# A graph network in four layers: layer 3's source factors by a way through DRAM instead of by two wide products per chunk

## The chip, the cores and the metric

The kernel runs on one core of a Trainium2 chip. The metric is the device time of one execution in microseconds (us); less is better. A core has five engines with their own instruction queues: TensorE (PE, the matrix products; PEld is its weight load), VectorE (DVE), ScalarE (ACT), GpSimd (POOL) and SyncE (SP), which here only issues transfers. An engine works off its own queue in order and waits for the others through semaphores.

## The reference

2708 nodes have 128 features each, and a sparse weighted adjacency of 2708 x 2708 in float32 with a full diagonal. Four layers each normalise the rows, cut them at 0, and add the layer's result to x. Layers 2 and 3 are those that matter:

```python
# layer 2
h = jnp.maximum(_layernorm(x), 0.0)
agg = adj @ h
msg = relu(agg @ W_msg.T + b_msg)
x = x + gru_cell(msg, h, W_ih, W_hh, b_ih, b_hh)
# layer 3
h = jnp.maximum(_layernorm(x), 0.0)
x_norm = _ln(h, g1, b1)
mask = (adj > 0) | eye
for i in range(2):
    hh = x_norm @ ff0_w[i].T
    s_src = hh @ attn_w[i, :c]
    s_dst = hh @ attn_w[i, c:]
    e = leaky_relu(s_src[:, None] + s_dst[None, :])
    e = where(mask, e, NEG)
    att = softmax(e, axis=1) @ hh + h
    att = _ln(att, g2, b2)
    h_next = h_next + elu(att @ ff1_w[i].T) / 2
x = x + h_next
```

With slope 0.01 the leaky ReLU is a maximum of two lines, so the exponential of a score splits into factors of source and destination. For source i and destination j the weight, up to a factor of i alone that the softmax takes out again, is mask x max(exp(-0.99 s_src[i]), exp(0.99 s_dst[j])) x exp(0.01 s_dst[j]). The kernel needs exp(-0.99 s_src[i]) along the free axis, the same on all 128 partitions, because there j lies on the partitions and i along the free axis. This is the tile `row`, the subject of the change.

## The kernel before

The 2708 nodes are 22 tiles of 128 (the last has 20). Layers 0 and 1 come first; layer 0 also writes the transposed adjacency to DRAM (`adjT`), and layer 1 works on lists of each node's neighbours. The changed part begins with layer 2.

Layer 2 goes over chunks of four tiles of destination nodes (`GROUPS`, six chunks, five of 512 columns and one of 148). `aggregate` (L941 to L963) takes a chunk's adjacency in five pieces of up to five row tiles, loads each with `nc.sync.dma_start` (L947, L949) into one of three buffers `a2`, makes from it the byte mask that layer 3 will use (L951 on VectorE, L954 on GpSimd), and adds its products up in PSUM (L959). So 22 products per chunk, five for each piece of 1.28 MB but two for the last. A buffer is free for the piece three later when its products and both masks have read it.

What else has to be done for a chunk is `finish_chunk` (L965 to L1060), a Python generator: the recurrent cell (L979 to L1009), its transposed result p_y (L1015), two normalisations (`moments`, `factors`, `scale_rows`), the transposed rows zT (L1034), then the source rows, then for each tile one product p_hv with `w_x` (L1050), which gives both heads' features and the four attention scores, with the exponentials of the destination scores (`hv`, `lift`), a copy of all four scores (`score`, used to flag sizes too large) and the scaled features (L1056).

The order of all instructions is written out by hand (`manual_schedule`). A software clock, `spend`, counts TensorE work, one unit for a product of 512 columns; `follow` enrols a generator, and `advance` resumes each at the point that its last `yield n` asked for, n units later. So the parts of chunk g's `finish_chunk` come to lie between the adjacency products of chunk g+1 and partly g+2, and each engine receives its instructions in the order in which Python emits them. This holds for SyncE too: a transfer stands in its queue where it was emitted, between the loads of pieces. The banks that `bank` hands out (p_h, p_z, p_m, p_row, p_hv, p_y) are two in turn.

The source rows before: `src_w` (L284) holds the source weights of a head copied along 128 columns, so that one product with zT gives the same source scores on all 128 partitions, and ScalarE writes their exponential to `row` (L1040 to L1045).

Layer 3's main part is `products` (L812): for each run of output tiles (`RUNS`: 3, 8, 8 and 3 tiles), each of the 22 source row tiles j and each head, `weigh` has VectorE make the weights from `row`, `lift` and `mask` (L806), and TensorE multiplies them (L838). The first run is interleaved with the last parts of `finish_chunk` for chunks 4 and 5; the part between the last adjacency product and the end of those chunks is called the seam below.

Layer 1 already uses a store followed by a read to all partitions: `pass_on` writes `passed` to DRAM (L443) and reads it back with `partition_broadcast` (L445).

Of the kernel before, what the change touches and what calls it, by code (L numbers as in the profile page):

```python
# [20 lines left out]
F32 = mybir.dt.float32  # L21
BF16 = mybir.dt.bfloat16
AF = mybir.ActivationFunctionType
# [7 lines left out]
P = 128  # L31
N = 2708
D = 128
# [18 lines left out]
def size(t):  # L52
    return min(P, N - t * P)
# [7 lines left out]
def listed_layers(ctx: ExitStack, tc: tile.TileContext, x, adj, w, out, flag):  # L61
    nc = tc.nc
# [4 lines left out]
    wdram = ctx.enter_context(tc.tile_pool(name="wdram", bufs=2, space=bass.MemoryType.DRAM))  # L67
    ps = ctx.enter_context(tc.tile_pool(name="ps", bufs=2, space=PSUM))

    def bank(name):  # L70
        return ps.tile([P, CH], F32, tag="ps", name=name)
# [12 lines left out]
    ident = const.tile([P, P], F32, name="ident")  # L84
# [60 lines left out]
    def span(t, k):  # L145

        return t * P, min(k * P, N - t * P)
# [12 lines left out]
    late = ctx.enter_context(tc.tile_pool(name="late", bufs=1))  # L160
# [36 lines left out]
    with tc.tile_pool(name="l0c", bufs=1) as fix:  # L197
# [4 lines left out]
        with (  # L202
# [6 lines left out]
            for gi, (g0, gk) in enumerate(GROUPS):  # L209
# [4 lines left out]
                for q in range(gk):  # L214
                    n = g0 + q
# [28 lines left out]
                for j in range(NT):  # L244
                    k = size(j)
                    p = bank("p_T")
# [34 lines left out]

    NX = 2 * D + 4
    w_x = late.tile([P, NX], F32, name="w_x")
    src_w = late.tile([P, 2, P], F32, name="src_w")  # L284

    def layer3_weights():
        nc.vector.tensor_copy(w_x[:, 0 : 2 * D], ff0T)
        for k in range(2):
            p = bank("p_w")[:, 0:2]
            nc.tensor.matmul(p, ff0[:, k, :], attn[:, 2 * k : 2 * k + 2], start=True, stop=True)  # L290
            nc.vector.tensor_copy(w_x[:, 2 * D + k : 2 * D + k + 1], p[:, 1:2])
            nc.vector.tensor_copy(w_x[:, 2 * D + 2 + k : 2 * D + 3 + k], p[:, 0:1])
        for k in range(2):
            nc.vector.tensor_copy(src_w[:, k, :], w_x[:, 2 * D + 2 + k : 2 * D + 3 + k].to_broadcast([P, P]))

# [470 lines left out]
    row = l3.tile([P, 2, N], F32, name="row")  # L768
    score = l3.tile([P, NT, 4], F32, name="score")
# [15 lines left out]
    def spend(units):  # L785
        clock[0] += units
# [147 lines left out]
    with (  # L934
# [30 lines left out]
        def finish_chunk(t0, k0, pa):  # L965

            c, n = span(t0, k0)
            u = n / CH
# [10 lines left out]
            p = bank("p_m")  # L979
# [31 lines left out]
            p = bank("p_y")  # L1011
# [21 lines left out]
            zT = zpool.tile([D, CH], F32, name="z3T")  # L1033
# [3 lines left out]
            )  # L1037
            spend(u)
            yield 2
            for k in range(2):  # L1040
                p = bank("p_row")
                nc.tensor.matmul(p[:, 0:n], src_w[:, k, :], zT[:, 0:n], start=True, stop=True)
                nc.scalar.activation(row[:, k, c : c + n], p[:, 0:n], AF.Exp, scale=-0.99)
                spend(u)
            yield 1  # L1045
            for q in range(k0):
                t = t0 + q
                m = size(t)
                p = bank("p_hv")
                nc.tensor.matmul(p[0:m, 0:NX], zT[:, q * P : q * P + m], w_x, start=True, stop=True)  # L1050
                spend(0.6)
                nc.scalar.activation(hv[0:m, t, :, D], p[0:m, 2 * D : 2 * D + 2], AF.Exp, scale=0.01)
                nc.scalar.activation(lift[0:m, t, :], p[0:m, 2 * D : 2 * D + 2], AF.Exp, scale=0.99)
                nc.scalar.copy(score[0:m, t, :], p[0:m, 2 * D : NX])
                for k in range(2):
                    nc.vector.tensor_scalar(  # L1056
                        hv[0:m, t, k, 0:D], p[0:m, k * D : (k + 1) * D], hv[0:m, t, k, D : D + 1], None, ALU.mult
                    )
                ready.add(t)
                yield 1  # L1060

        for g, (t0, k0) in enumerate(GROUPS):
            pa = accs.tile([P, CH], F32, tag=f"acc{g % 2}", name="p_agg")
            for j0 in range(0, NT, PIECE):
                aggregate(t0, k0, pa, j0)
            if t0 == 0:
                layer3_weights()
            follow(finish_chunk(t0, k0, pa))
            advance()
# [487 lines left out]
```

## Time and profile before

| | |
|---|---|
| time, median of 3 executions | 1110.71 us (1109.0 to 1111.08) |
| profiled execution, span | 1108.1 us |
| TensorE busy | 963.6 us (87%) |
| VectorE, ScalarE, GpSimd busy | 839.4, 504.2, 394.1 us |
| TensorE clock granted, mean | 0.933 |
| layer 2 with the source rows | about 646 to 811 us |
| seam | about 811 to 863 us |
| rest of layer 3 | about 863 to 1100 us |

The profile is that of one execution. "Busy" is the time in which an engine had an instruction at work; a product of float32 leaves two records. A wait is named by the instruction that ended it: "PE att L838 <- DVE wt L806" means that TensorE stood before the products of line 838 until VectorE's line 806 was done. PEclk is the granted share of TensorE's clock: at 0.50 each product takes twice as long. In a timeline each line has a start, a length, engine, line, operation, output and inputs, and in brackets the idle time ahead with what ended it. Since engines overlap, only the time before the engine that sets the pace counts.

### The profile page before, as it was taken

What the parts mean: (1) busy time and instruction counts of PE and PEld (TensorE: products, weight loads), DVE (VectorE), ACT (ScalarE), POOL (GpSimd) and SP (SyncE); (2) the same over time, 40 slices, a digit from 0 to 9 for tenths busy, and PEclk for the clock granted to TensorE, in tenths of its full rate; (3) what the DMA queues carried; (4) which work ended last, traced back from release to release, by engine and by line L of the source; (5) the groups of instructions that cost most, each with busy time, mean ns of one, the idle gap of its engine ahead of it and who ended that gap; (6) DMA issues with size and microseconds to landing.
All of it is one profiled execution on the core that took longest, in us unless ns stands there. A gap on an engine that the chain in (4) does not pass through costs nothing. (4 is left out here: it accounts for less than half of the span.)

```text
span 1108.1 us, 21904 instructions
## 1 busy us (share of the span) xinstructions
PE 963.6 (87%) x7968; PEld 760.1 (69%) x7968; DVE 839.4 (76%) x2948; ACT 504.2 (46%) x1319; POOL 394.1 (36%) x466
## 2 busy tenths in 40 slices
PE   3998887944389999999999979999979999999993
PEld 1455444523389999999898934444468899999772
DVE  5999999997766668676887255655578977997673
ACT  3857556623476666656676521433322200230142
POOL 4111111103385655776566253344310200340132
PEclk9999889755699999999999989999989999999996
DMA  9488978522133222322222056545300000000000
GB/s 361 164 299 281 324 259 288 178 64 68 46 106 102 96 86 90 106 86 101 83 103 80 28 193 209 190 157 198 100 18 1 1 9 1 1 20 1 2 15 14
DMA packets 55298, 125.39 MB, mean 113 GB/s; under 512 B 7414, under 2 KB 19782, under 8 KB 52472
## 3 DMA queue, kind: packets, MB, share of 16 engines
q1 hardware_dynamic: 48590, 121.12, 31.6%
q10 hardware_dynamic: 6590, 2.77, 1.0%
q8 instruction: 64, 1.05, 0.4%
q14 instruction: 54, 0.44, 0.1%
HBM read 77.30 MB, written 30.84 MB: 98 GB/s over the span
## 5 line engine op out<-in xcount | busy, mean ns | idle before, releaser
L838 PE MATMUL att<-hv,wt 128*128 128x129 f32 (+2 forms) x1936 | 240.7, 281 | 9.2 <-DVE wt L806 9.2
L838 PEld LDWEIGHTS att<-hv,wt 128*128 128x128 f32 (+2 forms) x1936 | 221.8, 190 | 26.2 <-DVE wt L806 9.1
L806 DVE SCALAR_TENSOR_TENSOR wt<-row,lift,mask 128x1024 f32<-128x1024 f32 (+5 forms) x176 | 160.0, 939 | 34.2 <-PE att L838 34.2
L423 POOL TENSOR_SCALAR put<-mine,value 128x128 f32<-128x128 bf16 x176 | 147.7, 855 | 72.4 <-DVE mine L339 70.0
L499 PE MATMUL p_m<-s,sel 128*128 128x128 bf16 x1452 | 160.8, 219 | 5.4 <-ACT g L511 5.4
L119 POOL TENSOR_TENSOR n_r<-n_r,minus_half 128x4 f32<-128x4 f32 (+1 forms) x36 | 51.3, 1425 | 316.1 <-DVE n_r L118 305.2
L503 PE MATMUL p_m<-d,cols 124*128 124x128 bf16 (+1 forms) x1452 | 161.0, 219 | 1.4 <-DVE cols L453 1.3
L220 PE MATMUL acc<-a,hs 128*128 128x512 f32 (+2 forms) x264 | 122.3, 599 | 27.6 <-DMA a<-in_adj 18.9
L524 PE MATMUL agg<-put,g 128*128 128x128 f32 (+1 forms) x968 | 135.8, 281 | 0.0
L241 DVE FIND_INDEX8 col<-val,a 128x8 uint16<-128x124 f32 (+1 forms) x441 | 118.6, 280 | 0.0
L959 PE MATMUL p_agg<-a,hs 128*128 128x512 f32 (+2 forms) x264 | 111.5, 564 | 7.7 <-DVE u L572 4.8
L524 PEld LDWEIGHTS agg<-put,g 128*128 128x128 f32 x968 | 118.1, 192 | 0.0
L499 PEld LDWEIGHTS <-sel 128*128 128x128 bf16 x1452 | 103.7, 97 | 10.8 <-issue 7.1
L503 PEld LDWEIGHTS <-cols 124*128 124x128 bf16 (+1 forms) x1452 | 101.8, 97 | 1.9 <-DVE cols L453 1.9
L240 DVE MAX8 val<-a 128x8 f32<-128x124 f32 (+1 forms) x441 | 102.6, 272 | 0.0
L511 ACT ACTIVATE g<-p_m 128x512 f32<-128x512 f32 x132 | 73.0, 553 | 63.6 <-PE p_m L503 63.6
L431 ACT ACTIVATE put<-mine,value 128x128 f32<-128x128 bf16 x308 | 100.5, 390 | 0.0
L220 PEld LDWEIGHTS acc<-a,hs 128*128 128x128 f32 (+1 forms) x264 | 49.7, 209 | 72.2 <-issue 43.4
L249 PEld LDWEIGHTS p_T<-ident,a 128*128 128x128 f32 x484 | 59.0, 146 | 52.8 <-ACT aT L253 25.4
L249 PE MATMUL p_T<-ident,a 128*128 128x128 f32 x484 | 77.7, 293 | 18.3 <-DMA a<-in_adj 10.0
L253 ACT ACTIVATE aT<-p_T 128x512 f32<-128x512 f32 (+2 forms) x132 | 70.9, 541 | 40.0 <-issue 16.3
L959 PEld LDWEIGHTS p_agg<-a,hs 128*128 128x128 f32 (+1 forms) x264 | 48.6, 196 | 56.6 <-issue 55.1
(228 smaller groups left out, 1396.6 us busy)
## 6 DMA issues: line engine op xcount, KB each, us to landing
a<-in_adj SPq DMA_DIRECT2D x21, 1354.0 KB
adjT<-aT SPq DMA_DIRECT2D x105, 256.0 KB
a<-adjT SPq DMA_DIRECT2D x20, 1280.0 KB
spread<-passed SPq DMA_DIRECT2D x22, 704.0 KB
later<-sel SPq DMA_DIRECT2D x22, 616.0 KB
later<-sel SPq DMA_DIRECT2D x22, 82.5 KB
adjT<-aT SPq DMA_DIRECT2D x21, 74.0 KB
a<-adjT SPq DMA_DIRECT2D x4, 370.0 KB
```

The costliest lines, as they stand in the source:

```text
L220: nc.tensor.matmul(accs[ci][:, 0:cw], h[0:m, n, :], a[0:m, c : c + cw], start=(n == 0), stop=(n == NT - 1))
L240: nc.vector.max(val[:, n, b, :], ab)
L241: nc.vector.max_index(col[:, n, b, :], val[:, n, b, :], ab)
L249: nc.tensor.transpose(p[0:k, q * P : q * P + m], a4[0:m, q, j * P : j * P + k], ident[0:m, 0:m])
L423: nc.gpsimd.tensor_scalar(st["put", 0][:, b, :], st["mine"][:, b, :], st["value"][:, b : b + 1], None, ALU.mult)
L431: nc.scalar.activation(st["put", 1][:, b - HP, :], st["mine"][:, b, :], AF.Identity, scale=st["value"][:, b : b + 1])
L499: nc.tensor.matmul(p[:, b - b0, :], st["sel"][:, b, :], s3[:, q, t % 2, :], start=(q == 0), stop=False)
L503: nc.tensor.matmul(p[:, b - b0, :], st["cols"][0:kb, b, :], d3[0:kb, b, q, :], start=False, stop=(q == 2))
L524: nc.tensor.matmul(agg, g[:, b - 4 * k, :], put, start=(b == 0), stop=False)
L806: nc.vector.scalar_tensor_tensor(wt[0:kj, :], row[0:kj, k, c : c + n], lift[0:kj, j, k : k + 1], mask[0:kj, j, c : c + n], op0=ALU.max, op ...
L838: nc.tensor.matmul(banks[s // 3][0:m, s % 3, :], wt[0:kj, q * P : q * P + m], hv[0:kj, j, k, :], start=(v < 2 and s // 3 not in touched), ...
L959: nc.tensor.matmul(pa[:, 0:n], h[0:k, j, :], a[0:k, j - j0, 0:n], start=(j == 0), stop=(j == NT - 1))
```

## The change

It no longer makes the source rows by products. `p_hv` gives the source scores of each node already, one node per partition, in `score`. The changed kernel takes their exponential for a whole chunk in one small operation (128 x 8), turns it by one transpose, copies it from PSUM, stores the 8 x 128 values to DRAM, and reads them back twice, once per head, to all 128 partitions. The `yield` lines set how far the steps lie apart on the software clock; the transfers go through SyncE's queue. The purpose is to take work off TensorE within layer 2. `src_w` and its copies are no longer needed.

```diff
@@ layer3_weights @@
-    src_w = late.tile([P, 2, P], F32, name="src_w")
...
-        for k in range(2):
-            nc.vector.tensor_copy(src_w[:, k, :], w_x[:, 2 * D + 2 + k : 2 * D + 3 + k].to_broadcast([P, P]))
@@ finish_chunk @@
             spend(u)
             yield 2
-            for k in range(2):
-                p = bank("p_row")
-                nc.tensor.matmul(p[:, 0:n], src_w[:, k, :], zT[:, 0:n], start=True, stop=True)
-                nc.scalar.activation(row[:, k, c : c + n], p[:, 0:n], AF.Exp, scale=-0.99)
-                spend(u)
-            yield 1
             for q in range(k0):
...
                 ready.add(t)
                 yield 1
+
+            own_e = zpool.tile([P, 8], F32, name="own_e")
+            nc.scalar.activation(
+                own_e[:, 0 : 2 * k0].rearrange("p (k t) -> p k t", k=2),
+                score[:, t0 : t0 + k0, 2:4].rearrange("p t k -> p k t"), AF.Exp, scale=-0.99,
+            )
+            yield 2
+            p = bank("p_row")
+            nc.tensor.transpose(p[0 : 2 * k0, 0:P], own_e[:, 0 : 2 * k0], ident)
+            turned = zpool.tile([8, P], F32, name="own_T")
+            nc.scalar.copy(turned[0 : 2 * k0, :], p[0 : 2 * k0, 0:P])
+            yield 2
+            passed = wdram.tile([8, P], F32, name="own_d")
+            nc.sync.dma_start(passed[0 : 2 * k0, :], turned[0 : 2 * k0, :])
+            yield 6
+            for k in range(2):
+                nc.sync.dma_start(
+                    row[:, k, c : c + n],
+                    passed[k * k0 : (k + 1) * k0, :].rearrange("t i -> (t i)")[0:n].partition_broadcast(P),
+                )
```

## The prediction

> **What bounds the kernel now.** I read the page's slices first, then busy time by stage, then TensorE's and SyncE's instructions in the stage the change touches, then who waits for whom. By stage (the window 646 to 811 us is layer 2 with the source rows; columns: length, then busy PE, PEld, DVE, ACT, POOL, granted clock, DMA share, GB/s):
>
> ```profile
> 646.00:811.00 165.00, 159.66 (x442) 76.27 (x442) 97.30 (x269) 54.14 (x140) 68.62 (x45) 0.97 0.51 170
> ```
>
> TensorE works 159.66 of 165 us, nothing else is over 60%, and DMA is half idle. The order of TensorE's work inside that stage (start, length, line, instruction, records; each f32 product leaves two records):
>
> ```profile
> 708.49 1.02 PE L959 MATMUL p_agg<-a,hs 128*128 128x512 f32 x2
> 709.35 1.88 PE L1042 MATMUL p_row<-z3T,src_w 128*128 128x512 f32 x4
> 711.07 1.02 PE L959 MATMUL p_agg<-a,hs 128*128 128x512 f32 x2
> ...
> 715.30 0.61 PE L1015 MATMUL p_y<-ident,y 128*128 128x128 f32 x4
> 715.74 1.02 PE L959 MATMUL p_agg<-a,hs 128*128 128x512 f32 x2
> 716.68 0.68 PE L1050 MATMUL p_hv<-w_x,z3T 128*128 128x260 f32 x2
> 717.19 13.04 PE L959 MATMUL p_agg<-a,hs 128*128 128x512 f32 x30
> ```
>
> From start to start a pair p_row (L1042) takes 1.72 us, one adjacency product (L959) 0.86 (15 from 717.19 to 730.07), one transpose 0.11 (four p_y in 0.44). So TensorE bounds this stage as long as the pieces of adjacency (1.28 MB, five products each) arrive in time. They all come through SyncE's queue, in order. Its waits (line, released by: total us, times, longest):
>
> ```profile
> SPq L947 <- PE p_agg L959: 92.6, 23, 13.5
> SPq L947 <- DVE mask L951: 48.0, 18, 17.1
> ...
> SPq L445 <- DMA passed<-where_T: 25.2, 22, 2.7
> ```
>
> The reader is to see that a load waits for a free buffer, in SyncE, and not for DMA: with three buffers it goes out two pieces ahead. The third line is a store read back through DRAM in layer 1, the pattern that the change adds: the read waits 25.2/22 = 1.1 us for the store.
>
> What a late piece costs is to be seen once, at the start of layer 2, where one load went out only when its buffer came free:
>
> ```profile
> 659.72 3.48 SPq L947 DMA_DIRECT2D a<-adjT  x2
> ...
> 665.70 8.13 PE L959 MATMUL p_agg<-a,hs 128*128 128x512 f32 x14 [2.85 <-DMA a<-adjT]
> 673.77 0.61 PE L290 MATMUL p_w<-attn,ff 128*128 128x2 f32 x4
> ...
> 667.00:670.00 3.00, 3.00 (x4) 1.10 (x4) 1.75 (x3) 0.18 (x1) 2.48 (x2) 0.51 0.86 330
> ```
>
> Issue at 659.72, first product at 665.70: 6.0 us. And the seven products after the 2.85 us gap took 8.07 us to the next start, not 7 x 0.86 = 6.02: 2.05 us more, with the clock at 0.51.
>
> **What the Trainium skill says.** DMA: Bandwidth & Descriptors, section Anatomy of one DMA: "any semaphore wait happens on the issuing sequencer before dispatch". It stands there for GpSimd's path; the waits of SyncE above show the same. TensorE: Matmul & The Clock Gate, section What's actually happening: after an idle window of some 3.4 us the clock is halved, and as long a busy window restores it. The trace agrees: 0.51 after a gap of 2.85 us, 0.50 for 816 to 820 us after one of 4.07 us. No price of the skill is used below, since the trace has each.
>
> **The change part by part.**
> *Removed products.* Two wide products per chunk, six chunks: 1.72 us each for chunks 0 to 4, 0.50 for the narrow chunk 5 (850.64 to 851.14). Chunks 0 to 3 lie in the TensorE-bound stage: 6.9 us. Chunks 4 and 5 lie in the seam after it: 2.2. The exponentials over 128x512 (0.60 us, ScalarE) and two copies (0.22, VectorE) fall away beside other work.
> *Added transposes.* Six of 0.11 us: 0.45 in layer 2, 0.2 in the seam. The two tiny ScalarE operations (0.17 and 0.25, by the rows of score and where_T) are hidden by adjacency products.
> *What the removal does not bring.* The head projections p_hv move up, but they share two banks, and p_y waits for the bank of the third. In the built program VectorE does hv of tiles 1 and 2, y three times (0.69 each), hv of 3 and 4, then p_y is possible. In chunk 0 a table load (1.28 us at 710.2) moves in front of the first hv as well. Step by step I get p_y at 716.2 and the next product's end at 717.5, against 718.05: 0.55 us gained, not 1.6. For the other three 1.45 to 1.8. So layer 2 gains 5.3 us, not 6.4.
> *Seam.* In the built order GpSimd does the last 20-row mask ahead of a power. Before, the first weights waited 1.48 us for that mask (814.92), and TensorE 4.07. I take 1.0 for this and 1.5 for the removed products, where VectorE is nearly as full as TensorE; together 2.5, bounds 0 and 4.
> *The added wait.* This decides. The order of SyncE's queue in the built program, for chunks 0, 1 and 2 alike: load of piece 1, store own_d, load of piece 2, both rows, load of piece 3. The store waits for ScalarE's own_T, that for the transpose, and the transpose stands on TensorE behind the second of piece 1's five products. So load 2, which now goes out two pieces ahead (at 701.4 for use at 720.65), is held until TensorE has done two fifths of piece 1. From the transpose's start T: 0.3 to ScalarE (its usual lag behind p_hv is 0.31), 0.25 its copy (where_T), then the store's issue 0.35: load 2 goes out at T+0.9, and its products can begin at T+6.9. TensorE has left 0.11 + 3 x 0.86 = 2.7 us in chunks 0 and 2, and 3.1 in chunk 1, where p_y comes after the transpose. It idles 4.2, 3.8 and 4.2: 12.2 us. Chunk 3's store comes after the last load, those of 4 and 5 in the seam, and nothing that is urgent stands behind them.
> *Clock.* Each gap is longer than the 2.85 us that halved the clock. Lost: 1.7 (3.4 us at half) to 2.2 (after the gap of 4.07, from 815.76 to 820.1); I take 2.0, three times 6.0.
> *The rows' own transfers.* 0.52 MB at the 390 to 417 GB/s that such a read has in layer 1: 1.3 us. With load 3 behind it, piece 3 is there at T+11.6 (6.9 + 1.3 + 1.28 MB in 3.4), and piece 2 is done at T+11.2 with a full clock, later with half: 0 to 0.4 us each, taken as 0. Chunk 0's rows are first read at 815 us, the others' behind 860: no reader waits.
> *Sum.* -5.3 - 2.5 + 12.2 + 6.0 = +10.4; 1110.7 + 10.4 = 1121.
>
> **Rivals.**
> *Stalls, but a full clock.* If the gaps fall so that no window is idle enough, 6.0 falls away: 1115. For it: a gap of 2.1 us at 308 left the clock alone. Against it: these are twice as long.
> *Deeper stalls.* Piece 3 comes late too, and VectorE, whose mask of piece 2 now stands ahead of the normalisation's factors, delays p_z: some 2 us per chunk more, 1127. For it: the factors do follow that mask in VectorE's order. Against it: I count p_z's input ready at T+17.3, while TensorE gets there at T+17.4 or later.
> *Faster: the wait is hidden.* If load 2 is not held, or lands before its use, only the gains stay: 6.4 + 2.0 + 1.5 for the mask = 9.9, 1101. For it: TensorE is the bound and DMA half idle, and load 2, out at 701.4, is due 13 us before its use. Against it: that slack is from issuing two pieces ahead, which the queue's order takes away, and one load needs 6.0 us where 2.7 remain.
>
> **How the numbers follow.** Forecast with half clock 0.60, full clock 0.20, deeper 0.08, hidden 0.12. Low end: idle 3.4 us thrice (a load in 5.2 us), no clock loss, all gains of 9.0: 1110.7 + 10.2 - 9.0 = 1112; I put 1110 to reach towards the hidden case. High end: 13 idle, 6.6 clock, 2 for piece 3, gains of 5: 1127. Faster: the hidden case, 0.12. Same: stalls that just cancel the gains, 0.04 out of the full-clock case. Slower: the rest, 0.84.
>
> **What would show it.** In the changed profile: no wide p_row; SyncE waiting for own_T three times within layer 2, each for many us, with a load right behind; TensorE idle 3.5 to 4.5 us before an adjacency product at about 720, 755 and 790, put down to the DMA of a; a clock near 0.5 after each; the next chunk with no such gap; the first weights earlier after layer 2. It is wrong if load 2 is seen out before the store, if it takes well under 6 us to its first product, or if the gaps are there but other waits of TensorE shrink by as much.

## The result, and the profile after

The kernel is slower: 1119.12 us (median of 4 executions, 1115.27 to 1120.13) against 1110.76 beside it, a ratio of 1.0072 with a 95% interval of 1.0045 to 1.0099. So the loss is 0.7%, small but clear of the noise. The forecast was 1121.

Look first at the adjacency products. This line of the page gives, after the bar, their busy time and mean length, and after the next bar the idle time ahead of them with what ended most of it; the first is the kernel before:

```profile
L959 PE MATMUL p_agg<-a,hs 128*128 128x512 f32 (+2 forms) x264 | 111.5, 564 | 7.7 <-DVE u L572 4.8
L956 PE MATMUL p_agg<-a,hs 128*128 128x512 f32 (+2 forms) x264 | 117.8, 588 | 19.5 <-DMA a<-adjT 14.8
```

The count is as before (264), but 14.8 us are spent waiting for a piece; 3.2 of them lie at the start of layer 2, where 2.8 lay before. The other 11.6 are new. TensorE's waits from 700 to 826 us (line, released by: total us, times, longest):

```profile
PE p_agg L956 <- DMA a<-adjT: 11.6, 3, 4.1
PE p_y L1012 <- DVE hv L1047: 0.5, 2, 0.3
PE p_hv L1041 <- DVE hv L1047: 0.5, 1, 0.5
```

Three gaps, one per chunk 0, 1 and 2. SyncE's waits from 640 to 830 us say why:

```profile
SPq L944 <- PE p_agg L956: 58.8, 14, 8.9
SPq L1065 <- ACT own_T L1062: 52.0, 3, 17.5
SPq L944 <- DVE mask L948: 40.3, 13, 17.1
...
SPq L1068 <- DMA own_d<-own_T: 3.3, 4, 2.0
```

The second line is new: three times the queue stood before the store of own_d, up to 17.5 us, until ScalarE had the transposed factors. The sums of the other two large lines are smaller than before, but that is no gain: these are waits of loads that stood in line anyway, and now stand behind the store. What went out when is in SyncE's timeline around the store of chunk 0 (start, length of the issue, line, transfer). In the kernel before, two loads left from 699.73 on (the second of them, the load of piece 2, at 701.35) and the next at 715.09:

```profile
699.73 1.97 SPq L947 DMA_DIRECT2D a<-adjT  x2
715.09 0.36 SPq L947 DMA_DIRECT2D a<-adjT  x1
```

In the changed kernel:

```profile
700.07 0.36 SPq L944 DMA_DIRECT2D a<-adjT  x1
717.91 0.29 SPq L1065 DMA_DIRECT2D own_d<-own_T  x1
718.36 0.37 SPq L944 DMA_DIRECT2D a<-adjT  x1
719.14 0.81 SPq L1068 DMA_DIRECT2D row<-own_d  x2
720.11 1.12 SPq L944 DMA_DIRECT2D a<-adjT  x2
```

Nothing leaves between 700.07 and 717.91; the load of piece 2 follows the store at once. TensorE's timeline has the other end of that load:

```profile
717.32 0.27 PE L1060 MATMUL p_row<-ident,own_e 128*8 128x128 f32 x1
717.43 2.74 PE L956 MATMUL p_agg<-a,hs 128*128 128x512 f32 x6
724.06 12.42 PE L956 MATMUL p_agg<-a,hs 128*128 128x512 f32 x24 [3.89 <-DMA a<-adjT]
736.41 0.66 PE L153 MATMUL p_z<-ident,z 128*128 128x128 f32 x4
...
758.38 12.62 PE L956 MATMUL p_agg<-a,hs 128*128 128x512 f32 x24 [3.62 <-DMA a<-adjT]
770.93 0.66 PE L153 MATMUL p_h<-ident,hs 128*128 128x128 f32 x4
...
793.43 13.56 PE L956 MATMUL p_agg<-a,hs 128*128 128x512 f32 x24 [4.08 <-DMA a<-adjT]
806.93 0.66 PE L153 MATMUL p_z<-ident,z 128*128 128x128 f32 x4
```

Issued at 718.36, first used at 724.06: 5.7 us, while TensorE had three products left. After each gap 12 products follow. At 0.86 us each they should take 10.3; from start to next start they took 12.35, 12.55 and 13.50. The windows show it (length, busy PE, PEld, DVE, ACT, POOL, clock, DMA share, GB/s):

```profile
720.00:724.00 4.00, 0.17 (x1) 0.00 (x0) 0.02 (x1) 0.00 (x0) 1.03 (x1) 1.00 0.94 335
724.00:727.00 3.00, 2.94 (x4) 1.40 (x5) 2.36 (x6) 0.43 (x2) 2.52 (x1) 0.50 0.93 338
...
793.00:799.00 6.00, 5.57 (x7) 2.45 (x8) 4.09 (x15) 1.65 (x4) 2.98 (x2) 0.50 0.98 334
```

In the first TensorE is empty and DMA full, with the late load, the row reads and the next loads under way at once. In the second and third TensorE is full again, at half the clock.

**Where the time went.** I measure between two points that every kernel here has: the first product of chunk 1's cell (p_m, at 702.43 before and 702.77 after) and the start of the last adjacency product (811.0 and 822.0). That stretch is 108.6 us before and 119.2 after: +10.7 (from unrounded times). Then the seam gives back 2.05: TensorE is 11.0 us later than before as the seam begins, 0.34 of it from before this stretch, and about 8.95 later once it is over, near the +8.4 of the medians. The profiled spans differ by only 5.4 (1108.1, 1113.5). Of the 3.5 us between, 1.5 lie in the rest of layer 3, where stretches at half clock fall differently (the section on the hardware shows them). The other 2.0 lie behind the issue of the last output transfer: from there to the end of the span it is 7.5 us before and 5.4 after, and 5.4 to 7.8 in the other runs, for a reason that no run here shows. Since both move the whole time of single executions, below the stage is given beside it: from the first to the last start of an adjacency product it is 164.3 us before and 174.9 after.

### The profile page after: what moved, and what is told of

It is laid out like the page before. It is cut to its first block, busy times and chain, and to the rows that moved or that the text cites. A ratio compares the mean times of both kernels' runs of the same rounds, so it can differ in the third digit from the quotient of the medians.

```text
span 1113.5 us, 21901 instructions
## 1 busy us (share of the span) xinstructions
PE 959.0 (86%) x7950; PEld 757.3 (68%) x7950; DVE 838.1 (75%) x2946; ACT 500.4 (45%) x1319; POOL 394.1 (35%) x466
## 5 line engine op out<-in xcount | busy, mean ns | idle before, releaser
L119 POOL TENSOR_TENSOR n_r<-n_r,minus_half 128x4 f32<-128x4 f32 (+1 forms) x36 | 48.2, 1339 | 306.6 <-DVE n_r L118 301.2
L220 PE MATMUL acc<-a,hs 128*128 128x512 f32 (+2 forms) x264 | 120.0, 589 | 29.1 <-DMA a<-in_adj 20.3
L956 PE MATMUL p_agg<-a,hs 128*128 128x512 f32 (+2 forms) x264 | 117.8, 588 | 19.5 <-DMA a<-adjT 14.8
```

The costliest lines, as they stand in the source:

```text
L220: nc.tensor.matmul(accs[ci][:, 0:cw], h[0:m, n, :], a[0:m, c : c + cw], start=(n == 0), stop=(n == NT - 1))
L956: nc.tensor.matmul(pa[:, 0:n], h[0:k, j, :], a[0:k, j - j0, 0:n], start=(j == 0), stop=(j == NT - 1))
```

## The experiments

Theory "hold": the store, in order in SyncE's queue, holds the load of piece 2, and the gaps and the slow clock after them are the whole loss. Rivals: "order" (the moved head projections and VectorE's new order cost the time), "traffic" (the row reads take DMA time from the loads), and "rows" (the row reads, waiting for the store, hold the loads). Before beside the first four runs was 1109.94 us (11 executions), beside the other three 1109.46 (10).

### The same transfers on ScalarE's queue

```
             passed = wdram.tile([8, P], F32, name="own_d")
-            nc.sync.dma_start(passed[0 : 2 * k0, :], turned[0 : 2 * k0, :])
+            nc.scalar.dma_start(passed[0 : 2 * k0, :], turned[0 : 2 * k0, :])
             yield 6
             for k in range(2):
-                nc.sync.dma_start(
+                nc.scalar.dma_start(
```

> The store and both row reads of the changed kernel are issued by ScalarE instead of SyncE; all else, the order on TensorE and VectorE too, stays. Theory (hold): the loss is the adjacency load held in SyncE's queue behind the store. Then SyncE never waits for own_T, the three gaps of 3.6 to 4.1 us before adjacency products go, and the clock loss behind them (some 6 us by the changed kernel's trace) too: 1119 - 11.6 - 6 = about 1101.5, range 1099 to 1104. Rival (order): the loss is from the moved head projections and VectorE's new order; nothing of that changes, so 1118 to 1119. Rival (traffic): the row reads take transfer time from the adjacency; the same bytes move, so 1117 to 1119.

Measured: 1104.64 us (1103.15 to 1105.52), ratio 0.9953 (0.9936 to 0.9969); stage 159.5. SyncE no longer waits for own_T:

```profile
SPq L944 <- PE p_agg L956: 88.8, 23, 11.1
...
SPq L944 <- DVE mask L948: 49.2, 19, 17.1
```

The three gaps are gone, the kernel is faster than before, and with the same transfers and products "order" and "traffic" fall. But I had expected some 3 us better, and the median lies just above the range. One gap of another kind stands in TensorE's timeline:

```profile
762.02 1.13 PE L956 MATMUL p_agg<-a,hs 128*128 128x512 f32 x2 [1.41 <-DMA a<-adjT]
```

The load that went out last before it left SyncE at 753.89, 8.1 us ahead; ScalarE had issued the two row reads just before it:

```profile
753.25 0.33 ACTq L1068 DMA_DIRECT2D row<-own_d  x1
...
753.61 0.45 ACTq L1068 DMA_DIRECT2D row<-own_d  x1
```

So this load, beside 0.52 MB of reads and from 759.11 on beside two more loads, took 2.4 us longer than the 5.7 above. That they shared the DMA engines is the likely reason; it was not tested by itself. The next run fits: there the same load leaves at 754.12 and the row reads only behind it, from 754.60 on, and its product starts at 760.67 without a wait. The gap's 1.4 us is half of what was missed, the rest is not located.

### The same queue, but the store later

```
             nc.scalar.copy(turned[0 : 2 * k0, :], p[0 : 2 * k0, 0:P])
-            yield 2
+            yield 12
             passed = wdram.tile([8, P], F32, name="own_d")
```

> The changed kernel with 12 instead of 2 units between the copy own_T and the store, so that the store stands behind the load of piece 4 in SyncE's queue, some two pieces later; still all on SyncE. Hold: SyncE comes to the store when own_T is done or nearly so and no load is late: 1101.5, range 1099 to 1104, no gap over 1 us before adjacency products. Order and traffic: as the changed kernel, 1117 to 1119.

Measured: 1099.57 us (1097.88 to 1101.96), ratio 0.9903 (0.9886 to 0.9919); stage 157.8. The best of all kernels here, with the store still on SyncE. Its queue's timeline (the view ends at 726, ahead of the second row read), then its waits:

```profile
700.69 14.81 SPq L944 DMA_DIRECT2D a<-adjT  x3
718.54 0.29 SPq L1065 DMA_DIRECT2D own_d<-own_T  x1
720.87 0.35 SPq L944 DMA_DIRECT2D a<-adjT  x1
...
725.58 0.52 SPq L1068 DMA_DIRECT2D row<-own_d  x1
```

```profile
SPq L944 <- PE p_agg L956: 87.3, 23, 11.4
...
SPq L1065 <- ACT own_T L1062: 7.7, 3, 3.0
```

Three loads leave before the store now, those of pieces 1 to 3; the store stands behind the load of piece 3, one place earlier than was put down. It waits 7.7 us in all instead of 52.0, at a point where the loads of pieces 2 and 3 are already out. TensorE goes through piece 2 without a stop (30 records are 15 products):

```profile
717.95 0.27 PE L1060 MATMUL p_row<-ident,own_e 128*8 128x128 f32 x1
718.06 13.23 PE L956 MATMUL p_agg<-a,hs 128*128 128x512 f32 x30
```

Ten units of spacing are worth 1119.12 - 1099.57 = 19.6 us, or 18.7 with each set against the kernel before that ran beside it. From chunk 1's p_m (703.39) to the last adjacency product (804.3) this kernel takes 100.9 us: 7.6 less than before, 18.3 less than the changed kernel.

### The wait alone, in the kernel before

The kernel before keeps its wide products and their order; at the end of `finish_chunk` the factors are computed, turned and stored as well. The store is never read; nothing of the computation is left out.

```
+            own_e = zpool.tile([P, 8], F32, name="own_e")
+            nc.scalar.activation(
+                own_e[:, 0 : 2 * k0].rearrange("p (k t) -> p k t", k=2),
+                score[:, t0 : t0 + k0, 2:4].rearrange("p t k -> p k t"), AF.Exp, scale=-0.99,
+            )
+            yield 2
+            p = bank("p_row")
+            nc.tensor.transpose(p[0 : 2 * k0, 0:P], own_e[:, 0 : 2 * k0], ident)
+            turned = zpool.tile([8, P], F32, name="own_T")
+            nc.scalar.copy(turned[0 : 2 * k0, :], p[0 : 2 * k0, 0:P])
+            yield 2
+            passed = wdram.tile([8, P], F32, name="own_d")
+            nc.sync.dma_start(passed[0 : 2 * k0, :], turned[0 : 2 * k0, :])
```

> The kernel before, with its wide row products kept and used, and the new exponential, transpose, copy and store added behind the head projections; no row is read back, so nothing uses the store. Hold: for chunks 1 and 2 the store stands before the load of piece 2 as in the changed kernel (gaps of about 4 us), for chunk 0 before the load of piece 3 (about 1.6 us): 10 us of gaps and 4 to 6 us of half clock on 1110.7, 1125, range 1120 to 1129. Order and traffic: neither the projections' place nor row reads are in it, so 1111 to 1112.

Measured: 1124.41 us (1123.46 to 1125.23), ratio 1.0133 (1.0117 to 1.015); stage 177.5. Its waits, of SyncE (640 to 830 us) and of TensorE (690 to 820 us):

```profile
SPq L1074 <- ACT own_T L1071: 57.4, 3, 19.4
```

```profile
PE p_agg L959 <- DMA a<-adjT: 9.2, 3, 4.0
```

Six stores of some kilobytes make the old kernel 14.5 us slower, with no read and no product moved. The stage is 13.2 longer: 9.2 of gaps (1.41, 3.98, 3.85), 0.3 of transposes, and a rest of 3.7 that goes with half a clock from 757.8 to 761.2 and from 792.0 to 798.8. Where the gap was only 1.41 us there was no half clock. In chunk 0 the store stands one place later, before the load of piece 3, and TensorE had six products or 5.4 us of work left when the transpose began, which is why that gap is small.

### Which of the two transfers

Only the store on ScalarE's queue, then only the row reads:

```
-            nc.sync.dma_start(passed[0 : 2 * k0, :], turned[0 : 2 * k0, :])
+            nc.scalar.dma_start(passed[0 : 2 * k0, :], turned[0 : 2 * k0, :])
```

> Only the store is issued by ScalarE, which has just made its data; the row reads stay on SyncE, now directly between the loads of pieces 2 and 3. Hold: load 2 is early again, but SyncE waits at the row reads until the store has landed, about 2 us behind the transpose, and load 3 stands behind them: three gaps of 2 to 3 us, now before piece 3, and perhaps the half clock: 1109, range 1105 to 1115. Order: 1118 to 1119. Traffic: 1117 to 1119.

```
             for k in range(2):
-                nc.sync.dma_start(
+                nc.scalar.dma_start(
```

> The counterpart of the run with the store on ScalarE: the store stays on SyncE, in front of the load of piece 2, and only the two row reads are issued by ScalarE. Hold: load 2 is held as in the changed kernel, three gaps of 3.6 to 4.1 us before piece 2 stay, and load 3 no longer has row reads in front of it in SyncE: 1118.5, range 1116 to 1120. If it is the row reads in SyncE's queue that matter and not the store: the gaps go, 1102 to 1105.

With the reads moved: 1117.92 us (1116.63 to 1120.09), ratio 1.0085 (1.0068 to 1.0102), stage 174.4, gaps 3.95, 3.33 and 3.82. Nothing changed: as long as the store is in the queue, the reads are not what hurts. With the store moved: 1113.46 us (1112.1 to 1115.72), ratio 1.0035 (1.0024 to 1.0045), stage 171.4. The hold is still there, but one place further back in the queue: now the reads wait there for the store's data,

```profile
SPq L1068 <- DMA own_d<-own_T: 55.5, 4, 17.1
```

and what stands behind them is the load of piece 3, five products further on:

```profile
717.38 7.03 PE L956 MATMUL p_agg<-a,hs 128*128 128x512 f32 x16
...
727.82 8.16 PE L956 MATMUL p_agg<-a,hs 128*128 128x512 f32 x14 [3.41 <-DMA a<-adjT]
```

So in the changed kernel "rows" would hold, had the store not held first. The gaps (3.41, 2.63, 3.35; 9.4 us) come to a little more than I had put for them.

### More and less of the same wait

```
-            yield 2
+            yield 3
             p = bank("p_row")
             nc.tensor.transpose(p[0 : 2 * k0, 0:P], own_e[:, 0 : 2 * k0], ident)
```

> Dose upwards: 3 instead of 2 units ahead of the transpose, so it stands one adjacency product later and two products are left to cover load 2 instead of three (in chunk 1 p_y changes sides too). Hold: each gap grows by 0.86 us, in chunk 1 by 1.3: gaps of about 4.75, 4.9 and 4.95, 14.6 us in place of 11.6; 1122, range 1120 to 1125. Order and traffic: no change, 1118 to 1120.

```
-            yield 2
+            yield 0
             p = bank("p_row")
             nc.tensor.transpose(p[0 : 2 * k0, 0:P], own_e[:, 0 : 2 * k0], ident)
```

> Dose downwards: no units ahead of the transpose, so it comes up to two products earlier, and four to five products with p_y are left to cover load 2. Hold: gaps of about 1.75, 1.9 and 2.8 us in place of 3.9, 3.6 and 4.1, and little or no half clock behind them, less about 1 us in all for TensorE waiting for own_e: 1111, range 1108 to 1115. Order and traffic: 1118 to 1120.

Later: the gaps grew to 4.61, 4.52 and 4.76, 13.9 us where 14.6 was worked out ahead, and the stage to 178.3, that is 3.4 more than in the changed kernel. The median did not follow: 1118.82 (1118.5 to 1122.71), ratio 1.0085 (1.0069 to 1.0102), about the changed kernel's. That is below the range of "hold" and within that of the rivals. The trace is of the slowest of the four executions (1122.71), that of the changed kernel of its fastest (1115.27), and outside the stage they differ by another 4 us. Whether the stage was as long in the three executions near 1118.7, and what made up for it, no trace shows. So the gaps and the stage of one execution support "hold" here, and the whole time does not.

Earlier: 1112.91 us (1110.42 to 1113.51), ratio 1.0026 (1.0015 to 1.0038), stage 170.2. TensorE's timeline:

```profile
716.57 0.27 PE L1060 MATMUL p_row<-ident,own_e 128*8 128x128 f32 x1 [0.26 <-DVE hv L1047]
...
723.62 4.56 PE L956 MATMUL p_agg<-a,hs 128*128 128x512 f32 x10 [2.35 <-DMA a<-adjT]
...
729.82 6.47 PE L956 MATMUL p_agg<-a,hs 128*128 128x512 f32 x14 [1.64 <-DMA a<-adjT]
```

The gaps before piece 2 shrank to 2.35, 1.73 and 2.10. I had not foreseen the second kind: before piece 3 in chunks 0 and 1 (1.64, 1.12), whose load stands behind the row reads. The changed kernel does not show it. The likely reason is that piece 2 takes longer there at half clock, so that piece 3 has landed by then; chunk 2 fits, where the clock was halved here too and the second gap is missing. In chunks 0 and 1 the clock stayed whole:

```profile
724.00:727.00 3.00, 3.00 (x8) 1.33 (x7) 2.27 (x8) 0.86 (x3) 2.18 (x1) 1.00 1.02 365
```

Eight records against four in the changed kernel's window of the same times. TensorE waits 8.9 us instead of 11.6 and has one stretch of half clock after a gap instead of three: 6.2 us between the medians, 4.9 with each set against the kernel before beside it, 4.7 in the stage.

## Why the forecast held, step by step

**The hold.** Shown: it goes when the queue goes (1104.64), when the store moves behind the loads (1099.57), it comes back alone in the kernel before (1124.41), and the gaps grow and shrink with the place of the transpose, though for the later transpose the median did not follow. By its terms, with T for the start of the transpose: load 2 goes out at T+1.04 (717.32 to 718.36) where T+0.9 was forecast; its first product is at T+6.74, 6.91 and 6.93 where T+6.9 was; TensorE had 2.85, 3.29 and 2.85 left where 2.7, 3.1 and 2.7 were. The gaps of 3.89, 3.62 and 4.08 sum to 11.6 against 12.2. The largest term was right because each of its pieces was read from a line of the kernel before: a store read back in layer 1, a load that had come late once, and the built order of the queue.

**The clock.** The 12 products after each gap took 2.0, 2.2 and 3.2 us more than at full clock, small waits included. Between the kernel with the store later and the changed one, the 18.3 us of the stretch are 11.6 of gaps and 6.7 of the rest, against 6.0 forecast. The third gap cost most because the clock stayed at half for 6.8 us (792.3 to 799.1), where I had 3.4 to 4.4.

**The gains in layer 2: the mis-sized term.** -5.3 forecast, -7.6 measured (the stretch before against that with the store later). Two parts of the missing 2.3 us can be named. I had chunk 0 gain 0.55 up to the next product; it gained 1.07 (the second product of piece 1 stands at 717.19 before and at 716.46 after, though the changed kernel ran 0.34 late). And I let p_y's waits for its bank stay, but they shrank: 1.4 us in the kernel before,

```profile
PE p_y L1015 <- DVE hv L1056: 1.4, 3, 0.9
```

all three after 740 us (0.24, 0.23 and 0.93), against one of 0.23 in that part of the changed one. Ahead of it the changed kernel has two new waits, 0.47 before p_hv and 0.25 before p_y, which the 1.07 includes. The line above is from 700 to 812 us. That makes 0.5 and 1.2 us; the remaining 0.6, spread over chunks 1 to 3, were not traced. My step-by-step count of VectorE's order was too strict: moving the projections up freed more than the products alone.

**The seam.** -2.5 forecast, -2.05 measured. The mask's share was near (the first weights are waited for 2.74 us, not 4.07, so 1.3 against 1.0). That leaves 0.7 for the removed products, where 1.5 had been put, and some 0.5 of it goes with the clock: TensorE's work there ran at half clock for 4.35 us before (815.76 to 820.11) and for 3.4 after (826.42 to 829.83). So their removal brought next to nothing in the seam: weights from VectorE are still waited for, 8.8 us in nine waits from 822 to 874 against 7.8 in seven from 811 to 863, that is 6.1 against 3.7 without the first one. That the seam's sum came near the forecast is in part luck.

**The row transfers.** Taken as nothing, and next to nothing they were in the changed kernel. That no reader waits was not quite so: VectorE stood 1.64 us at 870.62 until the last chunk's rows had landed, but TensorE's idle time there, 1.43 us, is hardly more than the 1.38 at the same place before. With a smaller gap they cost something, as the earlier transpose showed.

**The sum.** Forecast +12.9 by the end of layer 2 (gains -5.3, gaps 12.2, clock 6.0), measured +10.7; with the seam +10.4 against some +8.6; in the medians +8.4. The gains, larger than forecast by 2.3, are nearly the whole difference. Gaps (-0.6) and clock (+0.7) cancel, which is chance.

**The rivals.** "Hidden" was put at 1101, and that is what the kernel is once its load is not held: 1099.57. What spoke against it, the queue's order, decided. "Full clock" fell with the windows at 0.50. "Deeper stalls" did not come: p_z follows piece 3 with no wait. "Order" and "traffic", set up for the experiments, fell with the first two.

## What to carry to other kernels

An issuing queue is a resource like a buffer: before a transfer that waits for another engine goes into a queue, ask which loads stand behind it and how long before use they would have gone out. Emit such a store only when its data is sure to be ready, or behind loads for two pieces, or from a queue that carries no hurried loads; of what was tried, spacing was best here (1099.57; with both transfers on ScalarE's queue 1104.64, with only the store 1113.46), though layer 2 shows only 1.7 of the 5.1 us between the first two (stages of 157.8 and 159.5). And judge an idle gap on TensorE with its aftermath: three gaps of together 11.6 us cost 18.3.

## What the runs showed of the hardware

**Whether a gap halves the clock depends on its length and on where it falls.** The Trainium skill (TensorE: Matmul & The Clock Gate, section What's actually happening) says that the clock is halved after at least one idle window of some 3.4 us, and that the windows run freely, so that the phase counts. The prediction said that the trace agrees, but its gap of 2.85 us is shorter than that. The runs fit with a lower mark: gaps of 3.6 to 4.1 us were followed by half a clock each time in the changed kernel, one of 2.85 in the kernel before and one of 2.10 with the earlier transpose as well (0.51 from 790.3 to 793.7), while 1.12, 1.41, 1.64, 1.73 and 2.35 were not.

The phase accounts for the 2.10 and the 2.35. All changes of the clock in a run lie whole multiples of 3.41 us apart; in the changed kernel the stretches at half clock are 724.02 to 727.43, 758.15 to 761.56 and 792.28 to 799.11. In the run with the earlier transpose one stretch begins at 790.33. Counted back from there, a boundary falls at 722.07, within the gap of 2.35 (721.27 to 723.62), so that no window of 3.41 us holds more than 1.55 of it. The gap of 2.10 lies whole in the window that ends at 790.33. The gap of 2.1 us at 308, which the prediction names and which left the clock alone, is split in the same way by a boundary at 308.11. In the traces of all nine kernels, among the adjacency products of layer 2, each window at full clock with at least 2.04 us of idle TensorE was followed by half a clock, none with at most 1.85, and none lay between. This is no general mark: in the seam of the run on ScalarE's queue 1.13 us were enough.

**The clock is also halved where the trace shows no idle TensorE at all.** In the middle of layer 3, kernel before:

```profile
946.00:950.00 4.00, 4.00 (x24) 4.00 (x23) 3.81 (x14) 0.00 (x0) 0.00 (x0) 0.57 0.00 0
```

and the changed kernel, ten microseconds later at the same work, then 27 on (there 1.07 us of idle time before p_aT at 981.74 lie in the window ahead of the stretch, while before the stretch at 946 TensorE had been busy for two whole windows):

```profile
956.00:960.00 4.00, 4.00 (x39) 4.00 (x38) 3.83 (x15) 0.00 (x0) 0.68 (x1) 1.00 0.00 0
983.00:987.00 4.00, 4.00 (x22) 4.00 (x23) 3.83 (x15) 0.78 (x1) 0.04 (x1) 0.57 0.01 4
```

Busy is 4.00 of 4.00 in all three, and the records done are 24, 39 and 22. Such a stretch of 3.4 us costs about 1.6: over the one at 946 the lead of the kernel before shrinks from 8.97 to 7.32 us. They fall elsewhere from kernel to kernel. That section does not account for the one at 946, and no run here found its cause. They make up 1.5 of the 3.0 us by which the profiled spans differ less than the medians.
